# Layer norms of feed-forward and preparation in two stages, with three PSUM banks of their own for the centred values

## The chip, the cores and the metric

The kernel runs on one core of a Trainium2 chip. The metric is the device time of one execution in microseconds (us), as a median of several runs; lower is better. A core has five engines that run side by side, each through its own list of instructions in order: TensorE (PE in the profile, with its weight loads as PEld), VectorE (DVE), ScalarE (ACT), GpSimd (POOL) and SyncE (SP), which here issues all the DMAs. They meet at semaphores. Matrix products are written to PSUM, which has eight banks of 128 x 512 fp32 values; the other tiles lie in SBUF.

## What is computed

Four images of 128 channels and 64 x 64 pixels pass through four layers. The change concerns layer 2, an attention over the 4096 pixels ("tokens") of each image with 16 heads of 8 channels, with a layer norm ahead of it and a small feed-forward behind it:

```python
t = _to_tokens(x)
t = t + _L2_attn_ref(_ln_t(t), ...)

def _L2_attn_ref(x, rx_theta, ry_theta, w_comb, b_comb, w1, b1, w2, b2, g1, beta1, g2, beta2):
    qkv = _qz_ring(heads + rx_theta)          # cosines and their running products
    ...                                       # softmax attention of qkv with itself
    attn_out = ctx @ w_comb.T + b_comb
    x1 = _ln(x + attn_out, g1, beta1)
    zf = jnp.cos(x1[..., :NQ_FFN]) * jnp.cos(ry_theta)
    h = jax.nn.relu(zf @ w1.T + b1)
    ffn_out = h @ w2.T + b2
    return _ln(x1 + ffn_out, g2, beta2)
```

So each token has three norms over its 128 channels: one in preparation (`_ln_t`), two in the feed-forward (`g1`, `g2`).

## The kernel before

**Layout.** Channels lie on the 128 partitions and tokens along the free dimension. An image is worked in NCH = 8 chunks of CH = 512 tokens. A mean over the channels is therefore a matrix product: `layernorm_steps` (L99) multiplies the source by a centring matrix into a PSUM tile `ln_xc` (the source less its mean), squares that on ACT into `ln_sq` (L105), multiplies by a matrix of 1/128 into the PSUM tile `ln_var` (L108), and turns the variance with a 32 x 32 block transpose on DVE into `ln_vt` (L110), so that the square root on ACT (L112, `ln_sd`) and the reciprocal on DVE (L113) need only 16 values in a row. A second transpose spreads the result (`ln_rs`, L115), and DVE multiplies `ln_xc` by it (L118 without a gain, L120 with one; then POOL adds the shift at L121). `ln_xc` keeps its bank until that last product.

`layernorm_steps` is a generator with one `yield` between squaring and `ln_var`. `layernorm` (L92) runs it through at once. Layers 0 and 1 have norms of another kind, layer 3 calls `layernorm` too, in its own pools.

**The order of work.** For each of the four images there is a preparation (`prepare`, L913), the attention itself, and a feed-forward (`feed_forward`, L1223). The loop over b from 0 to 4 runs the feed-forward of image b-1 beside the preparation of image b, then the attention of image b. Both are lists of stages handed to `in_turn` (L797): turn i runs the last stage on the oldest chunk, then the one before it on the next chunk, and so on, with one `yield` after each call, so a chunk passes one stage per turn. `run` takes one call from the feed-forward and one from the preparation alternately.

- Preparation: `fetch` (loads a chunk, `x_in`), `norm` (the norm, and its store to DRAM), `products` (four transposes `tok_t`, the angles `phi`, a cosine of several DVE and ACT instructions into `cs`, and running products on POOL and DVE, L951 to L956), `store` (copies, four transposes `q_t`, splitting, stores). After the chunks, the first heads' queries and keys are loaded.
- Feed-forward: `fetch` (L1226: `den`, `num`, `nrm_in`), `attended` (transposes `den_t`, four DVE steps to a reciprocal, eight small products `rd_ps`, the product `att_ps`, the sum into `nrm_in` at L1256), `first_norm` (into `x1`), `cosines` (product `z_ps` and a cosine `zf`), `hidden` (four PSUM tiles `hid_ps` at once, four Relus at L1277), `sum_up` (eight products `ffn_ps`, the sum `res` at L1287), `last_norm` (norm into `blk`, sum with `x`, store at L1294).

**Buffers and the planner.** A tile pool has `bufs` buffers for each tag; a tile without a tag has its name as tag. For this stretch there is the SBUF pool `l2_mid` (two buffers each unless a tile says otherwise) and the PSUM pool `l2_ps` with eight banks, in which every tile has the tag "mm". In SBUF, `ln_sq` and `ln_vt` share the tag "ln_sq" and so two buffers. The calls set only priorities: a planner places the instructions in each engine's list when their inputs and buffers are there by its reckoning, the earlier in the program first. In the attention, whose pools follow, PE, DVE and POOL keep the written order instead. The attention's tiles take the memory that `l2_mid` leaves.

Of the kernel before, what the change touches and what calls it, by code (L numbers as in the profile page):

```python
# [9 lines left out]
F32 = mybir.dt.float32  # L10
# [5 lines left out]
PSUM = bass.MemoryType.PSUM  # L16

P = 128
# [3 lines left out]
CH = 512  # L22
# [7 lines left out]
class Common:  # L30
# [65 lines left out]
        for _ in self.layernorm_steps(out, src, work, psum, g, b):  # L96
            pass

    def layernorm_steps(self, out, src, work, psum, g=None, b=None):  # L99

        nc = self.nc
        xc = psum.tile([P, CH], F32, name="ln_xc", tag="mm")
        self.mm(xc, self.center, src)
        sq = work.tile([P, CH], F32, name="ln_sq")
        nc.scalar.activation(sq, xc, AF.Square)  # L105
        yield
        vp = psum.tile([P, CH], F32, name="ln_var", tag="mm")
        self.mm(vp, self.mean, sq)  # L108
        vt = work.tile([P, CH // 32, 32], F32, name="ln_vt", tag="ln_sq")
        nc.vector.transpose(vt.rearrange("p a b -> p (a b)"), vp)  # L110
        sd = work.tile([P, CH // 32, 1], F32, name="ln_sd")
        nc.scalar.activation(sd, vt[:, :, 0:1], AF.Sqrt, bias=self.eps5)  # L112
        nc.vector.reciprocal(sd, sd)  # L113
        rs = work.tile([P, CH // 32, 32], F32, name="ln_rs")
        nc.vector.transpose(rs, sd.to_broadcast([P, CH // 32, 32]))  # L115
        rs = rs.rearrange("p a b -> p (a b)")
        if g is None:
            nc.vector.tensor_tensor(out, xc, rs, ALU.mult)  # L118
        else:
            nc.vector.scalar_tensor_tensor(rs, xc, g, rs, ALU.mult, ALU.mult)  # L120
            nc.gpsimd.tensor_scalar(out, rs, b, None, ALU.add)  # L121
# [675 lines left out]
def in_turn(n, *stages):  # L797


    for i in range(n + len(stages) - 1):  # L800
        for k in reversed(range(len(stages))):
            if 0 <= i - k < n:
                stages[k](i - k)
                yield
# [20 lines left out]
def layer2_attention(K, xd, dpool, w):  # L825
# [6 lines left out]
    with ExitStack() as ctx:  # L832
# [81 lines left out]
        def prepare(b, big, two, work, psum):  # L914

            n = NTT * NH * (HD + 1)
            qt = big.tile([P, n + 32], F32, name="qt")
            nc.gpsimd.memset(qt[:, n:], 0.0)  # L920
            values = qt[:, 0:n].rearrange("p (h t d) -> p t h d", h=NH, d=HD + 1)
            nc.gpsimd.memset(values[:, :, :, HD : HD + 1], 1.0)
            shape = [P, 4, NH, HD]
            heads, xs, nrms, laters = {}, {}, {}, {}

            def fetch(c):
                xs[c] = work.tile([P, CH], F32, name="x_in", bufs=3)
                nc.sync.dma_start(out=xs[c], in_=xd[b][:, c * CH : (c + 1) * CH])

            def norm(c):  # L930
                nrms[c] = work.tile([P, CH], F32, name="nrm", bufs=3)
                K.layernorm(nrms[c], xs.pop(c), work, psum)
                nc.sync.dma_start(out=nrm_d[b % 2][:, c * CH : (c + 1) * CH], in_=nrms[c])

            def products(c):

                tp = psum.tile([P, 4, P], F32, name="tok_t", tag="mm")
                for j in range(4):
                    nc.tensor.transpose(tp[:, j, :], nrms[c][:, j * P : (j + 1) * P], K.ident)
                phi = work.tile(shape, F32, name="phi")  # L940
                nc.vector.tensor_tensor(
                    phi.rearrange("p t h d -> p (t h) d"),
                    tp.rearrange("p j (h d) -> p (j h) d", d=HD),
                    theta.unsqueeze(1).to_broadcast([P, 4 * NH, HD]),
                    ALU.add,
                )
                cs = heads[c] = work.tile(shape, F32, name="cs", bufs=3)
                K.cos(cs, phi, work, shape, "cos")
                cc = lambda d: cs[:, :, :, d : d + 1].rearrange("p t h o -> p (t h) o")
                q0 = work.tile([P, 4 * NH, 1], F32, name="q0")  # L950
                nc.gpsimd.tensor_tensor(q0, cc(1), cc(2), ALU.mult)  # L951
                for d in range(3, HD):
                    nc.gpsimd.tensor_tensor(q0, q0, cc(d), ALU.mult)
                for d in range(1, HD):
                    nc.vector.tensor_tensor(cc(d), cc(d - 1), cc(d), ALU.mult)
                nc.vector.tensor_copy(cc(0), q0)  # L956

            def store(c):

                cs = heads[c]  # L960
                nc.scalar.copy(values[:, 4 * c : 4 * c + 4, :, 0:HD], cs)
                j = c // 2
                if c % 2 == 0 and j < NJ - 1:
                    laters[j] = work.tile([P, NH, BT, HD], F32, name="later", bufs=1)
                if j < NJ - 1:
                    at = laters[j][:, :, 4 * (c % 2) : 4 * (c % 2) + 4]
                    nc.gpsimd.tensor_copy(at.rearrange("p h t d -> p t h d"), cs)
                if c % 2 and j < NJ - 1:
                    for q in range(4):
                        nc.sync.dma_start(  # L970
                            out=value_d[:, :, j, q].rearrange("h s t d -> s h (t d)"),
                            in_=laters[j][32 * q : 32 * q + 32].rearrange("s h t d -> s h (t d)"),
                        )
                tp = psum.tile([P, 4, P], F32, name="q_t", tag="mm")
                for j in range(4):
                    nc.tensor.transpose(tp[:, j, :], cs[:, j].rearrange("p h d -> p (h d)"), K.ident)
                tq = work.tile([P, CH], F32, name="tq", tag="phi")
                nc.scalar.copy(tq, tp.rearrange("p j t -> p (j t)"))
                rest = work.tile([P, CH], F32, name="rest", tag="cos_r")
                nc.vector.scalar_tensor_tensor(rest, tq, 4097.0, tq, ALU.mult, ALU.subtract)  # L980
                part = work.tile([P, 2, CH], F32, name="part")
                nc.vector.scalar_tensor_tensor(part[:, 0], tq, 4097.0, rest, ALU.mult, ALU.subtract)
                nc.gpsimd.tensor_tensor(part[:, 1], tq, part[:, 0], ALU.subtract)
                nc.sync.dma_start(
                    out=head_d[:, :, c * CH : (c + 1) * CH].rearrange("z q s -> q z s"), in_=part
                )

            first = []

            def stages():  # L990
                yield from in_turn(NCH, fetch, norm, products, store)
                first.extend(load(0, two))
                for t in first:
                    rounded(t)
                yield

            return stages(), qt, first
# [224 lines left out]

        def feed_forward(b, dsum, work, psum):  # L1223

            loads, x1s, hids, sums = {}, {}, {}, {}

            def fetch(c):
                cols = slice(c * CH, (c + 1) * CH)
                den = work.tile([2 * NH, CH], F32, name="den", bufs=3)
                nc.sync.dma_start(out=den, in_=den_d[:, :, cols].rearrange("p h f -> (p h) f"))  # L1230
                num = work.tile([P, 2, CH], F32, name="num", bufs=3)
                nc.sync.dma_start(out=num, in_=num_d[:, :, cols].rearrange("p q f -> q p f"))
                nrm = work.tile([P, CH], F32, name="nrm_in", bufs=4)
                nc.sync.dma_start(out=nrm, in_=nrm_d[b % 2][:, cols])
                loads[c] = num, den, nrm

            def attended(c):
# [17 lines left out]
                mm(ap, w_comb, num[:, 0])  # L1255
                nc.vector.scalar_tensor_tensor(at, ap, b_comb, at, ALU.add, ALU.add)  # L1256

            def first_norm(c):
                x1 = x1s[c] = work.tile([P, CH], F32, name="x1", bufs=4)
                K.layernorm(x1, loads[c][2], work, psum, g1, beta1)  # L1260

            def cosines(c):
                zp = psum.tile([P, CH], F32, name="z_ps", tag="mm")
# [15 lines left out]
            def sum_up(c):  # L1279
# [6 lines left out]
                r = sums[c] = work.tile([P, CH], F32, name="res")  # L1286
                nc.vector.scalar_tensor_tensor(r, fp, b2, x1s[c], ALU.add, ALU.add)  # L1287

            def last_norm(c):
                o = work.tile([P, CH], F32, name="blk")  # L1290
                K.layernorm(o, sums[c], work, psum, g2, beta2)
                x = loads[c]
                nc.gpsimd.tensor_tensor(x, x, o, ALU.add)
                nc.sync.dma_start(out=xd[b][:, c * CH : (c + 1) * CH], in_=x)  # L1294

            return in_turn(NCH, fetch, attended, first_norm, cosines, hidden, sum_up, last_norm)

        past = None
        for b in range(NB + 1):
            with (  # L1300
# [2 lines left out]
            ):  # L1303
                with (
                    tc.tile_pool(name="l2_mid", bufs=2) as work,
                    tc.tile_pool(name="l2_ps", bufs=8, space=PSUM) as psum,
                ):
                    parts = [feed_forward(b - 1, past, work, psum)] if b > 0 else []
                    if b < NB:
# [449 lines left out]
```

## Time and profile before

| | |
|---|---|
| median of 3 runs | 10960.34 us (10960.1 to 10969.78) |
| profiled execution | 10954.31 us, span 10952.5 us |
| PE busy | 9041.6 us, 83% of the span |
| DVE busy | 7656.5 us, 70% |
| ACT busy | 7514.8 us, 69% |
| POOL busy | 5233.6 us, 48% |
| attention's exponentials (ACT, L1204) | 4932.2 us in 5120 instructions |
| ln_var products, all layers | 240.2 us in 384 instructions, 182.9 us of PE idle before them |

The span is the time from the first to the last instruction of the profiled execution. Most of it, as the row of exponentials shows, is attention. Between its four phases lie the stretches of preparation and feed-forward. In the profile a matrix product of fp32 values appears as two PE instructions. A row of a wait table says which instruction stood idle until which other one was done; in a timeline the number in brackets is that idle time.

### The profile page before, as it was taken

To read this page: it belongs to the slowest core of one execution; us is meant where nothing else is said; L and a number is where in the kernel's file an instruction comes from. 1 tells how busy PE (TensorE), PEld (TensorE's weight loads), DVE (VectorE), ACT (ScalarE), POOL (GpSimd) and SP (SyncE) were. 2 spreads that over 40 slices of the span, in tenths; PEclk is the share of its full clock that TensorE was granted. 3 is DMA by queue.
4 is the path that set the end of the run, shared out by engine and by line. 5 is a ranking of instruction groups with operands and counts; after the bars stand their busy time and mean duration, and the time that the engine had idled before them with its cause. 6 is when DMAs were issued, how large, how long until landed. Compare 5 with 4: busy or idle time off the path is not lost. (4 is left out here: it accounts for less than half of the span.)

```text
span 10952.5 us, 184078 instructions
## 1 busy us (share of the span) xinstructions
PE 9041.6 (83%) x71952; PEld 3464.4 (32%) x71952; DVE 7656.5 (70%) x8462; ACT 7514.8 (69%) x10319; POOL 5233.6 (48%) x3143
## 2 busy tenths in 40 slices
PE   5777778777857999968999968999969999966767
PEld 2223323222332333323333323333323333323333
DVE  2788668668846777757777757777757777744563
ACT  2666565665527999958999948999948999932431
POOL 1565555556624666535665535665535655620000
PEclk8788878877878999979999979999979999977888
DMA  3322322322212222121221222212222212123004
GB/s 83 87 67 57 90 69 56 99 59 59 70 52 40 38 32 34 32 78 35 37 33 33 32 78 38 33 34 33 32 79 39 33 33 34 30 88 96 14 16 139
DMA packets 524327, 581.59 MB, mean 53 GB/s; under 512 B 106233, under 2 KB 329537, under 8 KB 520897
## 3 DMA queue, kind: packets, MB, share of 16 engines
q1 hardware_dynamic: 523456, 569.81, 22.6%
q8 instruction: 568, 9.31, 0.4%
q14 instruction: 303, 2.47, 0.1%
HBM read 373.96 MB, written 76.55 MB: 41 GB/s over the span
## 5 line engine op out<-in xcount | busy, mean ns | idle before, releaser
L1204 ACT ACTIVATE ex<-score 128x1024 f32<-128x1024 f32 x5120 | 4932.2, 1032 | 471.0 <-PE score L90 180.8
L90 PE MATMUL ctx_ps<-ex,qt 128*32 128x512 f32 x20480 | 2719.1, 595 | 0.0
L1151 POOL TENSOR_TENSOR folded<-ex 128x1024 f32<-128x1024 f32 x704 | 1679.4, 2386 | 2073.6 <-ACT ex L1204 2062.0
L1210 DVE STREAM_TRANSPOSE turned<-ex 128x1024 f32<-128x1024 f32 x1536 | 1879.5, 1224 | 470.1 <-ACT ex L1204 426.9
L90 PE MATMUL acc_ps<-turned,turned_v 128*32 128x256 f32 x24576 | 1826.3, 388 | 180.2 <-DVE turned L1190 177.4
L1190 DVE STREAM_TRANSPOSE turned<-ex 128x1024 f32<-128x1024 f32 x1536 | 1854.0, 1207 | 0.0
L90 PE MATMUL score<-queries,keys 32*128 32x512 f32 x10240 | 1359.9, 496 | 120.5 <-ACT ex L1204 74.3
L687 DVE TENSOR_TENSOR_SCAN hs<-decay,carry,hs 128x512 f32<-128x512 f32 x1024 | 1253.0, 1266 | 200.3 <-ACT decay L686 186.0
L686 ACT ACTIVATE decay<-dt,a_neg 128x512 f32<-128x512 f32 x1024 | 701.0, 689 | 788.0 <-DVE hs L687 764.3
L693 POOL TENSOR_TENSOR hs<-hs,c_sb 128x1024 f32<-128x1024 f32 x512 | 1204.9, 2374 | 46.1 <-DMA c_sb<-c_d 26.7
L90 PEld LDWEIGHTS score<-queries,keys 32*128 32x128 f32 x10240 | 524.7, 182 | 2176.5 <-issue 1664.1
L1152 POOL TENSOR_TENSOR quarters<-folded 128x512 f32<-128x512 f32 x704 | 905.1, 1286 | 55.2
L90 PEld LDWEIGHTS acc_ps<-turned,turned_v 128*32 128x32 f32 x24576 | 562.1, 108 | 897.0 <-issue 556.0
L90 PEld LDWEIGHTS ctx_ps<-ex,qt 128*32 128x32 f32 x20480 | 684.0, 110 | 461.0 <-DVE ctx L1133 53.2
L683 DVE TENSOR_TENSOR hs<-dtx,b_ps 128x2048 f32<-128x2048 f32 x256 | 582.2, 2274 | 256.6 <-PE b_ps L90 173.4
L90 PE MATMUL y_ps<-hs,pair 128*64 128x512 f32 x2048 | 644.2, 752 | 137.3 <-POOL hs L693 137.2
L1133 DVE COPY ctx<-ctx_ps 128x512 f32<-128x512 f32 x256 | 177.0, 691 | 669.6 <-PE ctx_ps L90 663.2
L690 POOL COPY carry<-hs 128x4 f32<-128x4 f32 x256 | 59.3, 232 | 1019.7 <-DVE hs L687 976.8
L1023 POOL TENSOR_TENSOR turned_v<-v,quarter 128x1024 f32<-128x1024 f32 x192 | 459.2, 2392 | 18.1 <-DMA v<-value_d 18.1
L1197 DVE TENSOR_REDUCE dacc<-quarters 128x2 f32<-128x512 f32 x704 | 453.4, 644 | 8.0 <-POOL quarters L1152 8.0
L90 PE MATMUL ln_var<-ln_sq,mean 128*128 128x512 f32 x384 | 240.2, 710 | 182.9 <-ACT ln_sq L105 158.1
L90 PE MATMUL b_ps<-dbc,spread 32*128 32x512 f32 x512 | 319.4, 706 | 70.7 <-DVE hs L683 70.7
(353 smaller groups left out, 9684.3 us busy)
## 6 DMA issues: line engine op xcount, KB each, us to landing
c_sb<-c_d SPq DMA_DIRECT2D x512, 128.0 KB
queries<-head_d SPq DMA_DIRECT2D x1024, 64.0 KB
keys<-head_d SPq DMA_DIRECT2D x1024, 64.0 KB
dt<-dt SPq DMA_DIRECT2D x128, 256.0 KB
dtx<-dtx SPq DMA_DIRECT2D x128, 256.0 KB
w<-in_L_ffn_weight SPq DMA_DIRECT2D x32, 1024.0 KB
w<-in_L_ffn_weight SPq DMA_DIRECT2D x128, 256.0 KB
under<-xp SPq DMA_DIRECT2D x384, 66.0 KB
```

What stands on the lines that cost most here:

```text
L90: self.nc.tensor.matmul(out, lhsT, rhs, start=start, stop=stop)
L683: nc.vector.tensor_tensor(hs, dtx2, bb.unsqueeze(1).to_broadcast([P, NQ, CH]), ALU.mult)
L686: nc.scalar.activation(ex, dt2[:, q, :], AF.Exp, scale=a_neg[:, q, g : g + 1])
L687: nc.vector.tensor_tensor_scan(hs[:, q, :], ex, hs[:, q, :], carry[:, g, q : q + 1], ALU.mult, ALU.add)
L693: nc.gpsimd.tensor_tensor(at, at, cs.unsqueeze(1).to_broadcast([P, 2, CH]), ALU.mult)
L1023: nc.gpsimd.tensor_tensor(t, v.unsqueeze(2).to_broadcast([P, 4 * BT, 4, HD]), quarter.unsqueeze(1).to_broadcast([P, 4 * BT, 4, HD]), ALU.mult,
L1151: nc.gpsimd.tensor_tensor(hs, exs[:, :, 0], exs[:, :, 1], ALU.add)
L1152: nc.gpsimd.tensor_tensor(qs, hs[:, :, 0 : CH // 2], hs[:, :, CH // 2 :], ALU.add)
L1190: nc.vector.transpose(*upright)
L1197: nc.vector.tensor_reduce(at, qs, AX.X, ALU.add)
L1204: nc.scalar.activation(ex, sps[p], AF.Exp, scale=scale, accum_out=dacc[:, j, h, t : t + 1] if summed else None)
L1210: nc.vector.transpose(*upright)
```

## The change

Both norms of the feed-forward and the one of the preparation become two stages. The first, one turn earlier, makes `ln_xc` and `ln_sq` and stops at the generator's `yield`; the second takes the generator up and does the rest. Preparation has five stages instead of four, the feed-forward nine instead of seven. `ln_xc` gets a tag "xc" with three buffers in these norms, and the pool's default falls from eight banks to five, so the tag "mm" keeps five. `ln_sq` gets three buffers in these norms, and `ln_vt` a tag of its own with the pool's default of two, in layer 3's norm as well. `num` falls from three buffers to two.

```diff
-    def layernorm_steps(self, out, src, work, psum, g=None, b=None):
+    def layernorm_steps(self, out, src, work, psum, g=None, b=None, tag="mm", bufs=None):
-        xc = psum.tile([P, CH], F32, name="ln_xc", tag="mm")
+        xc = psum.tile([P, CH], F32, name="ln_xc", tag=tag, bufs=bufs)
         self.mm(xc, self.center, src)
-        sq = work.tile([P, CH], F32, name="ln_sq")
+        sq = work.tile([P, CH], F32, name="ln_sq", bufs=bufs)
         nc.scalar.activation(sq, xc, AF.Square)
         yield
         vp = psum.tile([P, CH], F32, name="ln_var", tag="mm")
         self.mm(vp, self.mean, sq)
-        vt = work.tile([P, CH // 32, 32], F32, name="ln_vt", tag="ln_sq")
+        vt = work.tile([P, CH // 32, 32], F32, name="ln_vt")
...
+            def centred(c):
+                nrms[c] = work.tile([P, CH], F32, name="nrm", bufs=3)
+                halves[c] = K.layernorm_steps(nrms[c], xs.pop(c), work, psum, tag="xc", bufs=3)
+                next(halves[c])
+
             def norm(c):
-                nrms[c] = work.tile([P, CH], F32, name="nrm", bufs=3)
-                K.layernorm(nrms[c], xs.pop(c), work, psum)
+                next(halves.pop(c), None)
                 nc.sync.dma_start(out=nrm_d[b % 2][:, c * CH : (c + 1) * CH], in_=nrms[c])
...
-                yield from in_turn(NCH, fetch, norm, products, store)
+                yield from in_turn(NCH, fetch, centred, norm, products, store)
...
-                num = work.tile([P, 2, CH], F32, name="num", bufs=3)
+                num = work.tile([P, 2, CH], F32, name="num", bufs=2)
...
+            def first_centred(c):
+                x1 = x1s[c] = work.tile([P, CH], F32, name="x1", bufs=4)
+                halves[c] = K.layernorm_steps(x1, loads[c][2], work, psum, g1, beta1, tag="xc", bufs=3)
+                next(halves[c])
+
             def first_norm(c):
-                x1 = x1s[c] = work.tile([P, CH], F32, name="x1", bufs=4)
-                K.layernorm(x1, loads[c][2], work, psum, g1, beta1)
+                next(halves.pop(c), None)
...
+            def last_centred(c):
+                sums[c] = sums[c], work.tile([P, CH], F32, name="blk")
+                lasts[c] = K.layernorm_steps(sums[c][1], sums[c][0], work, psum, g2, beta2, tag="xc", bufs=3)
+                next(lasts[c])
+
             def last_norm(c):
-                o = work.tile([P, CH], F32, name="blk")
-                K.layernorm(o, sums[c], work, psum, g2, beta2)
+                next(lasts.pop(c), None)
+                o = sums[c][1]
                 x = loads[c]
...
-            return in_turn(NCH, fetch, attended, first_norm, cosines, hidden, sum_up, last_norm)
+            return in_turn(NCH, fetch, attended, first_centred, first_norm, cosines, hidden, sum_up, last_centred, last_norm)
...
-                    tc.tile_pool(name="l2_ps", bufs=8, space=PSUM) as psum,
+                    tc.tile_pool(name="l2_ps", bufs=5, space=PSUM) as psum,
```

More of the change, by code (lines that the diff above doesn't have):

```diff
@@ L923, in prepare @@
             shape = [P, 4, NH, HD]
-            heads, xs, nrms, laters = {}, {}, {}, {}
+            heads, xs, nrms, laters, halves = {}, {}, {}, {}, {}
             def fetch(c):
@@ L1223, in feed_forward @@
         def feed_forward(b, dsum, work, psum):
-            loads, x1s, hids, sums = {}, {}, {}, {}
+            loads, x1s, hids, sums, halves, lasts = {}, {}, {}, {}, {}, {}
             def fetch(c):
```

## The prediction

> **What bounds the kernel now.** I read the page first. No engine is full over the span (PE 83%, DVE 70%, ACT 69%), and TensorE's granted clock dips to 7 tenths between the long attention phases. There lie the stretches that the change touches, so I asked next for the busy times of each of the five: preparation alone (3185 to 3346), three stretches of feed-forward beside preparation, and feed-forward alone (9609 to 9797).
>
> ```profile
> core 0: us, PE busy (x) PEld busy (x) DVE busy (x) ACT busy (x) POOL busy (x), PEclk, DMA share, GB/s
> 3185.00:3346.00 161.00, 42.49 (x97) 18.62 (x97) 71.25 (x148) 55.69 (x76) 37.44 (x68) 0.56 0.31 79
> 4707.30:4982.30 275.00, 164.18 (x422) 72.42 (x422) 148.05 (x290) 116.32 (x172) 83.67 (x99) 0.74 0.31 85
> 6343.50:6619.00 275.50, 163.84 (x424) 72.13 (x424) 149.73 (x291) 118.13 (x174) 83.18 (x99) 0.76 0.30 86
> 7978.40:8251.00 272.60, 160.47 (x424) 70.73 (x425) 150.64 (x291) 118.28 (x174) 83.11 (x100) 0.76 0.28 87
> 9609.20:9797.00 187.80, 126.54 (x320) 52.54 (x320) 85.98 (x147) 70.75 (x105) 45.80 (x34) 0.77 0.26 83
> ```
>
> Together 1172 us, 10.7% of the span. In a mixed stretch PE works 164 of 275 us and nothing else works longer: it is a chain of waits. The wait table of PE for the first mixed stretch says which:
>
> ```profile
> PE ln_var L90 <- ACT ln_sq L105: 36.7, 24, 8.3
> PE rd_ps L90 <- DVE rc L1248: 30.1, 8, 6.7
> PE q_t L976 <- DVE cs L955: 21.0, 3, 8.5
> PE att_ps L90 <- DVE num L1253: 6.9, 8, 1.3
> PE den_t L1242 <- DMA den<-den_d: 6.7, 1, 6.7
> ```
>
> The columns are total us, times, longest. All 24 norms of the stretch stop PE between their two products. The same row has 35.7 and 33.5 us in the next two mixed stretches, 21.6 (16 times) in feed-forward alone, 12.1 (8 times) in preparation alone: 139.6 us in all. The timeline shows the worst one:
>
> ```profile
> 4768.36 1.02 PE L90 MATMUL ln_xc<-x_in,center 128*128 128x512 f32 x2
> 4777.71 2.08 PE L90 MATMUL ln_var<-ln_sq,mean 128*128 128x512 f32 x2 [8.33 <-ACT ln_sq L105]
> ```
>
> Between the two PE does nothing, though other products were ready. Why? Following PE through 4713 to 4880, its products come exactly in the order of the calls in the program. In layer 3 the same planner leaves that order for one tile only:
>
> ```profile
> 10406.53 1.02 PE L90 MATMUL ln_xc<-x,center 128*128 128x512 f32 x2
> 10407.39 0.83 PE L90 MATMUL kv_sum<-v,e_k 128*128 128x129 f32 x6
> 10408.30 1.12 PE L90 MATMUL ln_var<-ln_sq,mean 128*128 128x512 f32 x2
> ```
>
> kv_sum has a bank of its own and fills the gap; tiles of the tag "mm" never pass one another. So I read the plan as first come, first served within a tag: a product of tag "mm" waits until all earlier ones have their bank. Last, does a stretch's end set the next start? Yes: attention's first exponential waits for the feed-forward's last store.
>
> ```profile
> 4981.06 1.28 ACT L1204 ACT_TABLE_LOAD   x1 [8.46 <-DMA xd<-x]
> ```
>
> **What the Trainium skill says.** "TensorE: Matmul & The Clock Gate", Part 1, has the array at half clock by default and at full clock only after some 3.4 us of sustained work; the trace agrees, since att_ps takes 1141 ns after the rd_ps gap where the same shape takes 592 at best. "PSUM — Partial Sum Buffer", The four PSUM rules: one matmul output fills at most one of eight banks; all tiles here are a bank, so three kept for centred values leave five. "ScalarE: Activation LUTs", What ACT_TABLE_LOAD costs: 1283 ns and a drain of about 1380; the trace has the 1283, but the next instruction starts 1.30 us after the load (4773.52, 4774.82), so I use 1.28. "Perfetto Trace Analysis", Optimization Strategy, warns that repeated bubbles can mean that no buffer is left for the next tile; before, PE shows no wait for a bank, and that is what the change puts at stake.
>
> **The change part by part.** Arithmetic and instruction counts stay; order and buffers move. My sums are against the profiled execution (10954.3, span 10952.5 and 1.8 outside), 6 us below the median of the runs.
>
> *Split of the norm.* In each turn ln_xc and ln_sq now come one turn ahead of ln_var, so ln_var's input is old when PE reaches it. The gates of the expert layers are already split like that; there the wait is at most 0.8 us (5.4 us over 7 waits from 9828 to 9868). Removed in a mixed stretch: 36.7, 35.7, 33.5, mean 35. What is late next is q_t for cs: of the ln_var waits in the two stretches that now end in such a wait (from tok_t at 4817.9 and 4860.5 to q_t) about 3 us come back. Net -32.
>
> *Tag of its own for xc.* ln_xc leaves the "mm" order and goes when its input and one of three banks are there. I listed the calls: every bank is released by a norm call before its next user, but at five of the 24 places (preparation's chunks 4, 6, 7, feed-forward's 5, last norm of 1) only one to three calls before. There PE may meet an ln_xc whose bank DVE has not yet released. From below nothing, from above 2 us each; I take +4. On the other side, ACT and DVE stand in line behind norms that wait: from 4818 to 4830 the cosine chain lost 1.0 (L201 behind ln_sq), 0.8 (L204 behind ln_vt) and 2.6 us (Abs behind a second ln_sq and a table load). With two or three such places a stretch, -6.
>
> *Five banks for all else.* hidden takes four in 1.1 us of PE; they come free with the four Relus, 2.42 us on ACT, starting 1.0 to 2.1 us after hid's first product (4760.7 to 4762.8, 4837.7 to 4839.8). ffn_ps is freed by 0.75 us on DVE. So the second product after hid waits about 1 us, in a chunk. Bounds 0 and 7 (below, rival three). I take 0.75 times 8, +6.
>
> *More turns.* Preparation has 12 turns instead of 11, feed-forward 16 instead of 14. The last chunk's chain (ffn, res, ln_xc, ln_sq, ln_var) is as long as before; filling costs at most one short turn of 8.4 us (the tail's from 4951.8 to 4960.0). I take +4.
>
> *Clock.* ln_var's mean is 775 ns against 592; half of 48 times 0.18 is on the path: -4. att_ps stays slow, for its rd_ps gap stays.
>
> *num with two buffers.* Loads already start when att_ps frees a buffer (4720.72, 4738.47) and land 3.9 us later, a turn ahead of use. One chunk less ahead still leaves more than 10 us: 0. SP's queue holds the same loads behind the same event, so x_in, den and nrm_in behind it on SP meet nothing new. If the cover went, each would cost up to 3.9 us.
>
> *ln_sq three deep, ln_vt with its own two.* It frees the next ln_sq from the older ln_vt; counted in the -6. Layer 3's norm gets it too, 32 times in some 360 us, on an order that PE already fills: 0, at most 3 either way. x, now held one turn longer with three buffers, loads at the latest two turns ahead: 0.
>
> Sum, mixed: -32 + 4 - 6 + 6 + 4 - 4 = -28, three times -84. Feed-forward alone: -21 for its waits, +4 banks, +2 turns, -2 clock: -17; rd_ps (15.1) stays. Preparation alone: its path is tok_t to cs to q_t (12.0 us of a period of 13.6, 3214.7 to 3226.7); of 12.1 us nearly all is beside it, and what goes is tok_t's wait for L118, 8 times 0.5: -4. Total -105: 10849 for the profiled execution, **10855** as a median, 1.0% less.
>
> **The rivals.**
> *One, more than the waits.* If free-running ln_xc also draws rd_ps and q_t forward and the clock holds, 40% of the other 58 us of rd_ps, q_t and att_ps goes: mixed -51, alone -28 and -12: 190 in all, 10770. For it: DVE is only 54% busy in a mixed stretch. Against it: rd_ps needs four DVE steps after den_t, at least 1.75 us.
> *Two, it comes back.* PE's order around the norms may stay (each ln_xc held by its bank until just before its ln_var), or q_t and rd_ps take up the whole gain, DVE's order being what limits: 10950. For it: q_t already has 8.5 us waits. Against: most ln_var waits lie in turns that end without one.
> *Three, slower.* One mechanism: head of line at five banks. If hid's Relus stand on ACT behind a Sin and two table loads with a square root (1.28 + 0.72 + 1.28 + 0.32 = 3.6) and then take 2.42, PE stops some 6 to 7 us a chunk. At 7 in the mixed stretches (56 in place of 6: -28 becomes +22) and 5 in the last (40 in place of 4: +19): 66 + 19 - 4 = +81, 11041. It decides from 34/8 = 4.3 us a chunk. For it: hidden, ffn_ps, tok_t can want six banks at once. Against: Relus start within 2.1 us in the turns I looked at, and the norms held up to three of the eight banks before as well.
>
> **How the numbers follow.** Chances: forecast 0.57, one 0.15, two 0.09, three 0.19. The forecast's own range, with the bounds above (waits regained to 70 or 100%, banks 0 to 1.5 us a chunk, turns 0 to 8), is 10790 to 10920. The whole range must leave out no more than two in ten: half of rival one below 10770, most of rival three above 10975. A measurement here can tell a change of about 0.2%, 22 us. Faster: 0.57 and 0.15, nothing more: 0.72. Same: most of two, 0.08. Slower: 0.20.
>
> **What would show it.** Right: the row ln_var from ln_sq falls below 8 us in each mixed stretch; ln_xc stands apart from its ln_var in PE's order; mixed stretches of 240 to 255 us, the last near 170, the first within 8 of 161. Wrong: rows of PE waiting for ACT hid L1277 (banks) above 30 us a stretch; ln_xc waiting for L118 or L120 above 10; q_t's row grown from 21 to over 45; a stretch not shorter though the ln_var row is gone.

## The result and the profile after

The changed kernel takes 10844.95 us (median of four runs, 10833.8 to 10850.65), the kernel before 10965.06 us beside it (four runs, 10960.1 to 10977.47): a ratio of 0.9891, with a 95% interval of 0.9879 to 0.9903. A second set gave 10836.52 against 10959.83, 0.9892 (0.9876 to 0.9908). The profiled span fell from 10952.5 to 10847.5 us.

To compare stretches I cut every trace at the same events: preparation alone from the last store of the layer before, the others from attention's last reduction (`dsum`), up to attention's first exponential table load, and the last stretch up to layer 3's first load of `x`. Lengths in us, with PE's busy time in it after the slash:

| | layers 0 and 1 | preparation alone | mixed 1 | mixed 2 | mixed 3 | feed-forward alone | what follows it |
|---|---|---|---|---|---|---|---|
| before | 3179.0 | 168.0 | 273.7 / 164.2 | 272.5 / 163.2 | 269.6 / 159.8 | 186.7 / 126.5 | 1156.7 |
| after | 3193.1 | 163.3 | 244.4 / 153.3 | 245.2 / 155.7 | 245.6 / 155.6 | 152.9 / 111.7 | 1155.8 |

The five stretches give 119.0 us back. Layers 0 and 1, whose code is the same, took 14 us longer in this one profile. They vary like that: 3178.8 to 3193.1 over the 14 profiles of this study. The four attention phases take 1360 to 1363 us each, before and after.

The busy times of the changed kernel by stretch (us of the window, then its length, busy time and number of instructions of each engine, PE's granted clock, DMA share and rate):

```profile
core 0: us, PE busy (x) PEld busy (x) DVE busy (x) ACT busy (x) POOL busy (x), PEclk, DMA share, GB/s
3193.14:3356.47 163.33, 41.38 (x102) 20.87 (x102) 69.92 (x161) 53.59 (x74) 39.21 (x68) 0.57 0.33 92
4717.46:4961.81 244.35, 153.29 (x422) 71.47 (x422) 148.48 (x290) 114.80 (x172) 84.68 (x99) 0.76 0.34 96
6324.39:6569.56 245.17, 155.71 (x422) 72.33 (x422) 147.55 (x290) 114.69 (x171) 83.93 (x99) 0.75 0.33 96
7931.55:8177.19 245.64, 155.57 (x422) 72.45 (x422) 147.76 (x290) 114.75 (x172) 83.55 (x99) 0.75 0.34 96
9538.83:9691.75 152.92, 111.66 (x320) 48.66 (x320) 83.28 (x146) 69.96 (x105) 45.77 (x32) 0.84 0.32 100
```

DVE and ACT do the same work in less time; their sums hardly move. PE has as many instructions as before, but in feed-forward alone it is busy 14.9 us less, at a clock of 0.84 instead of 0.77. The rest of the gain is idle time of PE (length less busy time): in the first mixed stretch 109.5 us before, 91.1 after; in feed-forward alone 60.1 and 41.3. PE's wait table for the first mixed stretch says what went and what came:

```profile
PE ln_xc L90 <- DVE ln_rs L120: 24.3, 7, 6.2
PE q_t L980 <- DVE cs L959: 20.5, 4, 7.0
PE rd_ps L90 <- DVE rc L1252: 10.4, 6, 3.7
PE ln_xc L90 <- DVE nrm L118: 6.9, 3, 5.9
...
PE hid_ps L90 <- ACT zf L206: 2.9, 2, 2.2
PE q_t L980 <- ACT hid L1285: 0.7, 1, 0.7
```

The row of ln_var waiting for ln_sq, 36.7 us before, has shrunk to one wait of 0.7 us. A new pair has come instead: ln_xc waits for L118 and L120, the last reads of an older centred value, so for a bank, 31.2 us in ten places. The row of rd_ps has fallen from 30.1 to 10.4, that of q_t stands where it was. The bank wait that rival three was built on, PE held by hid's Relus (now L1285), is 0.7 us.

The timeline of PE has the largest new wait:

```profile
4774.07 1.95 PE L90 MATMUL ln_var<-ln_sq,mean 128*128 128x512 f32 x4
4775.86 1.02 PE L90 MATMUL ln_xc<-nrm_in,center 128*128 128x512 f32 x2
4776.82 0.43 PE L1246 MATMUL den_t<-ident,den 32*128 32x32 f32 x4
4783.45 2.08 PE L90 MATMUL ln_xc<-x_in,center 128*128 128x512 f32 x2 [6.20 <-DVE ln_rs L120]
4785.32 1.91 PE L90 MATMUL rd_ps<-ident,rc 128*128 128x128 f32 x8
```

Two norms' ln_var come together without any wait: their ln_sq are a turn old. Then PE stands for 6.2 us at an ln_xc that waits for its bank. But look at what comes behind it. rd_ps needs rc, and DVE's timeline shows when that was made:

```profile
4782.65 0.75 DVE L120 SCALAR_TENSOR_TENSOR ln_rs<-ln_xc,g,ln_rs 128x512 f32<-128x512 f32 x1
4783.31 0.54 DVE L1250 RECIPROCAL rd<-rd 128x64 f32<-128x64 f32 x1
4783.89 0.57 DVE L1252 COPY rc<-rd 128x512 f32<-128x512 f32 x1
```

The bank came free at 4783.40 and rc was ready at 4784.46. With a free bank, PE would still have stopped at rd_ps until then, for about as long. Much of the 31 us, then, may be the old wait for rc under another name. Whether it is, the experiments had to say.

### The profile page after: what moved, and what is told of

It reads as the page before. It is cut to its first block, busy times and chain, and to the rows that moved or that the text cites. A ratio compares the mean times of both kernels' runs of the same rounds, so it can differ in the third digit from the quotient of the medians.

```text
span 10847.5 us, 184105 instructions
## 1 busy us (share of the span) xinstructions
PE 9021.2 (83%) x71952; PEld 3473.1 (32%) x71952; DVE 7647.7 (71%) x8462; ACT 7513.2 (69%) x10317; POOL 5239.0 (48%) x3143
## 5 line engine op out<-in xcount | busy, mean ns | idle before, releaser
L1208 ACT ACTIVATION_READ_ACCUMULATOR ex<-score 128x1 f32 x1664 | 348.7, 210 | 0.0
```

Of the source, the lines that this page charges most:

```text
L1208: nc.scalar.activation(ex, sps[p], AF.Exp, scale=scale, accum_out=dacc[:, j, h, t : t + 1] if summed else None)
```

## The experiments

The runs e1 to e4 shared one chip, e5 to e11 another, e12 ran on a third, always beside the kernel before. Theory A: each wait of PE costs its length, so the bank waits cost up to 31 us a mixed stretch. Theory B: the gain comes from the tag, which lets ln_xc leave the order of the calls. Theory C: in a mixed stretch the bank waits lie mostly where PE would wait for rc or cs anyway. The lengths, in us (the totals of e1 to e6 are single executions):

| | what differs | mixed 1, 2, 3 | feed-forward alone | total |
|---|---|---|---|---|
| before | | 273.7, 272.5, 269.6 | 186.7 | 10953 to 10965 |
| after | | 244.4, 245.2, 245.6 | 152.9 | 10844.95 |
| e1 | split, eight banks of one tag | 252.5, 251.3, 253.4 | 165.6 | 10876.2 |
| e2 | four banks and four | 246.6, 248.6, 246.2 | 156.2 | 10844.5 |
| e3 | tag, no split | 250.0, 248.9, 252.8 | 176.3 | 10886.4 |
| e4 | x four buffers | 237.5, 238.9, 238.5 | 152.6 | 10836.9 |
| e5 | buffers alone | 267.7, 265.4, 269.0 | 186.4 | 10946.6 |
| e6 | e4, preparation as before | 243.2, 241.3, 242.8 | 158.3 | 10848.7 |
| e7 | e4, preparation's xc in "mm" | 247.4, 248.3, 249.4 | 152.7 | 10856.4 |
| e11 | e4, attended split | 223.1, 218.2, 218.8 | 133.4 | 10746.8 |
| e12 | e11, q_t a turn later | 215.0, 213.1, 211.6 | 134.6 | 10710.8 |

**e1: the split without the banks.** All tiles in eight banks of the tag "mm", the rest of the change kept.

```diff
-halves[c] = K.layernorm_steps(x1, loads[c][2], work, psum, g1, beta1, tag="xc", bufs=3)
+halves[c] = K.layernorm_steps(x1, loads[c][2], work, psum, g1, beta1, tag="mm", bufs=None, sqs=3)
...
-tc.tile_pool(name="l2_ps", bufs=5, space=PSUM) as psum,
+tc.tile_pool(name="l2_ps", bufs=8, space=PSUM) as psum,
```

> The changed kernel's three-stage split with all PSUM tiles in one tag of eight banks again (squares keep three buffers). Theory A (the split alone brings the gain, and the three separate banks cost some 31 us of PE waits for L118 and L120 in each mixed stretch): ln_xc's waits for a bank fall from 31 to under 8 us a mixed stretch, ln_var's stay under 5, mixed stretches 225 to 240 us against 245 of the changed kernel. Theory B (free-running ln_xc in its own tag brings the gain): ln_xc sits in the order of calls again and mixed stretches go back to 260 to 273. Theory C (the waits for a bank only stand where PE would wait for cs or rc anyway): 245 within 3, with the rows of q_t and rd_ps grown by what ln_xc loses. Feed-forward alone: A and C 150 to 156, B 165 to 185.

No bank wait is left, and the mixed stretches are not shorter but 7 us longer than with the change. PE's wait table for the first of them:

```profile
PE rd_ps L90 <- DVE rc L1252: 34.0, 8, 6.5
PE q_t L980 <- DVE cs L959: 33.0, 6, 10.6
PE att_ps L90 <- DVE num L1257: 7.1, 7, 2.3
```

The 31 us of bank waits are back as 23.6 us more for rc and 12.5 more for cs. So they were not a cost on top: theory A falls on the banks. C has the direction, but the stretches lie above its 245 within 3, and feed-forward alone, 12.7 us longer than with the change, is in B's range: leaving the order of the calls is worth something by itself.

**e2: four banks and four.** As the change, with four banks for centred values and four for the rest; ln_sq stays at three buffers.

```diff
-halves[c] = K.layernorm_steps(x1, loads[c][2], work, psum, g1, beta1, tag="xc", bufs=3)
+halves[c] = K.layernorm_steps(x1, loads[c][2], work, psum, g1, beta1, tag="xc", bufs=4)
...
-tc.tile_pool(name="l2_ps", bufs=5, space=PSUM) as psum,
+tc.tile_pool(name="l2_ps", bufs=4, space=PSUM) as psum,
```

> The changed kernel with four banks for centred values and four for all else. Theory A: ln_xc's waits for L118 and L120 fall from 31 to under 12 us a mixed stretch; hidden needs all four other banks, so PE waits for Relus of L1285 and for ffn_ps, 8 to 25 us; mixed stretch 238 to 252, feed-forward alone 155 to 170. Theory C: ln_xc's waits fall but the stretch gains nothing even where no new wait for Relus comes, 245 to 260.

The bank waits of ln_xc fell only to 17.1 and 5.8 us, not below 12, rd_ps's wait rose to 15.6, and the stretches are 0.5 to 3.5 us longer. That lies in the ranges of A and of C, so it doesn't part them; it shows that one bank more for centred values, taken from the rest, gains nothing.

**e3: the banks without the split.** The tag with three banks as in the change, each norm in one stage again, in preparation too.

```diff
-in_turn(NCH, fetch, attended, first_centred, first_norm, cosines, hidden, sum_up, last_centred, last_norm)
+in_turn(NCH, fetch, attended, first_centred, cosines, hidden, sum_up, last_centred)
```

> The changed kernel's banks and buffers, but the norms in one stage again (preparation of four stages, feed-forward of seven). Theory B: the tag alone lets ln_xc go early, so ln_var's waits stay under 10 us and the mixed stretch at 245 within 5. Theory A: ln_xc is freed by a bank only shortly before its ln_var, so waits of ln_var and ln_xc together stay at 30 us or more and the mixed stretch is 258 to 275, feed-forward alone 165 to 185.

The row of ln_var fell to 5.3 us in the first mixed stretch with no split at all: with a bank of its own, ln_xc leaves the order of the calls by itself, and its ln_sq is early. In feed-forward alone 10.1 us of the row stay. The mixed stretches, 249 to 253 us, are at the top of B's 240 to 250 and above it; feed-forward alone, 176.3, is in A's range. Tag and split are two ways to the same end in a mixed stretch; alone, the stretch needs the split.

**e4, e8, e10: four buffers for x.** In the mixed stretches of the change one thing is late that was not before, and its place is the very end. The timeline of the changed kernel there (SPq is SP's DMA queue):

```profile
4942.59 1.89 POOL L912 CAST keys<-keys 128x2048 fp32r<-128x2048 f32 x1
...
4944.43 1.90 POOL L912 CAST queries<-queries 128x2048 fp32r<-128x2048 f32 x1
4944.64 1.12 PE L90 MATMUL ln_var<-ln_sq,mean 128*128 128x512 f32 x2 [0.69 <-ACT ln_sq L105]
...
4946.29 1.26 POOL L1306 TENSOR_TENSOR x<-x,blk 128x512 f32<-128x512 f32 x1
...
4947.57 6.11 SPq L1307 DMA_DIRECT2D xd<-x  x3
...
4954.44 0.46 SPq L1289 DMA_DIRECT2D x<-xd  x1
4954.95 0.66 SPq L903 DMA_DIRECT2D keys<-head_d  x1
4958.09 1.26 POOL L1306 TENSOR_TENSOR x<-x,blk 128x512 f32<-128x512 f32 x1 [4.75 <-issue]
4959.38 0.32 SPq L1307 DMA_DIRECT2D xd<-x  x1
...
4961.81 1.28 ACT L1208 ACT_TABLE_LOAD   x1 [14.93 <-DMA xd<-x]
```

From the last ln_var to attention's table load it takes 17.2 us, in all three mixed stretches. In the kernel before it took 10.6 to 10.7, here up to the table load at 4981.06:

```profile
4970.36 1.13 PE L90 MATMUL ln_var<-ln_sq,mean 128*128 128x512 f32 x2 [0.75 <-ACT ln_sq L105]
```

The x of the last chunk is loaded only at 4954.44, ten microseconds after its norm's ln_var, behind the stores of the three chunks before it (4947.57 to 4953.68), the first of which frees its buffer, because x is held one turn longer now. POOL has a part in it: the first of those stores follows a sum (4946.29) that stands behind the casts of the first heads' keys and queries for attention. The last chunk's sum, its store and attention's first exponential wait for the late x. The edit gives x a fourth buffer and takes the room from den:

```diff
-x = loads[c] = work.tile([P, CH], F32, name="x", bufs=3)
+x = loads[c] = work.tile([P, CH], F32, name="x", bufs=4)
...
-den = work.tile([2 * NH, CH], F32, name="den", bufs=3)
+den = work.tile([2 * NH, CH], F32, name="den", bufs=2)
```

> The changed kernel with x in four buffers (den gets two to make room). If the last chunk's late load of x (issued 4954.44, behind two stores, its sum at 4958.09) is what lengthens the end, attention's first exponential comes 5 to 7 us sooner after the last ln_var (17.2 us now, 10.7 before the change): mixed stretches 238 to 240 us, feed-forward alone 153 within 2, preparation alone unchanged. If another thing holds the end (the stores' place on SP, POOL's casts), mixed stretches stay at 245 within 2.

Each mixed stretch became 6.2 to 7.1 us shorter. Feed-forward alone stayed: there the change, too, loads the last x (9676.55) ahead of its last three stores (from 9682.98). In the timeline of e4 the last loads of x are out early:

```profile
4935.91 1.35 SPq L1289 DMA_DIRECT2D x<-xd  x3
...
4944.63 1.13 PE L90 MATMUL ln_var<-ln_sq,mean 128*128 128x512 f32 x2 [0.69 <-ACT ln_sq L105]
...
4947.51 1.89 POOL L912 CAST keys<-keys 128x2048 fp32r<-128x2048 f32 x1
...
4949.35 1.89 POOL L912 CAST queries<-queries 128x2048 fp32r<-128x2048 f32 x1
4951.20 1.26 POOL L1306 TENSOR_TENSOR x<-x,blk 128x512 f32<-128x512 f32 x1
...
4958.88 1.28 ACT L1208 ACT_TABLE_LOAD   x1 [12.02 <-DMA xd<-x]
```

The tail is 14.3 us in each mixed stretch, 2.9 less than after and still 3.6 more than before, because the two casts have moved behind the last ln_var and the last three sums follow them. It is 14.3 in every run with the casts in that place (e7, e8, e10 and e12 too); in e11 both lie ahead of it again, and it is 11.6.

So less than half of e4's gain is the tail; 3.8 us on average lie ahead of the last ln_var. PE's 422 instructions come in the same order in both kernels. In the first mixed stretch, counted from its start, e4 is 1.3 us ahead at one q_t, whose cs is ready sooner. Another 2.3 us come at the products some 20 us later, from an att_ps to an ln_var, which take longer in the change (the att_ps 1.06 us against 0.59). The other two stretches show the same two steps. The late load of x does not explain them; their cause stays open.

Since one execution can't carry 8 us, it was timed again, and then beside the changed kernel on one chip:

> The kernel of e4 again, in rounds: the change with x four buffers and den two. The theory that x's three buffers delay the last chunk by some 6.5 us in each mixed stretch: 10820 to 10838, ratio to before 0.9870 to 0.9888, and below the change's 10845. The rival that e4's single look was luck: 10842 to 10850.

> The changed kernel itself, on the same chip as the next two: 10840 to 10850 us, ratio to before 0.988 to 0.990.

> The kernel of e4 and e8 beside the changed one. If x's fourth buffer is worth the 6.5 us of each mixed stretch that its timeline shows: 10822 to 10834, 12 to 22 us below the run of the changed kernel in this call, mixed 237 to 240. If the difference between e8 and the change was that of two chips: within 6 us of the changed kernel.

e8 gave 10826.98 (ratio 0.9876, 0.986 to 0.9893). In the last set the changed kernel (e9) took 10836.52 (10830.3 to 10848.01) and the one with four buffers (e10) 10819.38 (10811.83 to 10826.48): 17 us less, every run of it below every run of the other, and within the 12 to 22 expected. Both medians lie some 3 us below the ranges expected for them. The three mixed stretches are 25.6 us shorter together in these two profiles, preparation alone 3.8 and feed-forward alone 2.7 longer. The tail gives 2.8 of the 8.5 us of a stretch.

**e5: the buffers alone.** The kernel before, with ln_sq three deep, ln_vt with its own two, and num with two.

```diff
-sq = work.tile([P, CH], F32, name="ln_sq")
+sq = work.tile([P, CH], F32, name="ln_sq", bufs=bufs)
...
-vt = work.tile([P, CH // 32, 32], F32, name="ln_vt", tag="ln_sq")
+vt = work.tile([P, CH // 32, 32], F32, name="ln_vt")
...
-num = work.tile([P, 2, CH], F32, name="num", bufs=3)
+num = work.tile([P, 2, CH], F32, name="num", bufs=2)
```

> The kernel before with only the changed buffers: ln_sq three deep, ln_vt with two of its own, num with two; norms whole, all tiles in eight banks of one tag. Theory A (the buffers give nothing by themselves; the gain is the split and the tag): mixed stretches 268 to 275 us, feed-forward alone 184 to 189, the ln_var row of PE 35 to 38 us in the first mixed stretch, total within 12 us of before. Theory B (ln_vt in line for ln_sq's buffers holds the norms back, as my term of -6 a stretch had it): mixed 262 to 267, feed-forward alone 178 to 183, total 25 us less.

Between the two: the mixed stretches lost 6.1, 7.1 and 0.6 us, 4.6 on average, and feed-forward alone nothing. ln_var's row in the first mixed stretch shows where it came from, 36.7 before:

```profile
PE ln_var L90 <- ACT ln_sq L105: 26.3, 24, 3.8
```

A cost of num's third buffer doesn't show, but it was not taken away alone, so a small one could hide in the gain of the others. With e5 as the base, split and tag can be told apart. Averages of the three mixed stretches: split -14.9 (e1), tag -16.8 (e3), both -22.3 (after). Feed-forward alone: -20.7, -10.1 and -33.5. They overlap in the mixed stretches, where preparation runs beside the feed-forward, and add up where it does not.

**e6 and e7: preparation taken out of the three banks.** Both have x's fourth buffer, so they stand against e4. In e6 preparation's norm is whole, in "mm"; in e7 it is split, in "mm".

```diff
-halves[c] = K.layernorm_steps(nrms[c], xs.pop(c), work, psum, tag="xc", bufs=3)
+halves[c] = K.layernorm_steps(nrms[c], xs.pop(c), work, psum, sqs=3)
```

> Only the feed-forward's norms are split and use the three banks of their own; preparation's norms are whole in the other five; x has four buffers, den two, as in e4. Theory C (preparation's norms gain only because they are off the order of the calls; their wait comes back): PE's ln_var row 10 to 14 us in the first mixed stretch, mixed 243 to 250 against 238 of e4, feed-forward alone 152 to 154, preparation alone 166 to 169, total 10850 to 10870. Theory D (two kinds of norm taking turns for three banks cost as much as the split of preparation's gains): ln_xc's bank waits fall from 31 to under 10 us and mixed stays at 235 to 240, total 10825 to 10840.

> Both norms split, but preparation's centred values in the five banks in order of the calls, only the feed-forward's in the three; x four buffers, den two. Theory D (mixing two kinds of norm in the three banks costs): ln_xc's bank waits fall below 12 us and mixed to 230 to 235, total 10815 to 10830. Theory C (bank waits lie where PE would wait for cs and rc anyway): mixed 237 to 243, the q_t and rd_ps rows take up what the ln_xc rows lose, total 10833 to 10850.

In e7 the bank waits fell to 5.1 us, as wanted, and the mixed stretches grew by 10 us; rd_ps waits 34.6 us there. Theory D, that two kinds of norm in three banks cost, is wrong. C has the direction, but its 237 to 243 was too good: e7 also takes the free order from preparation's ln_xc. That this order is worth those 10 us is not shown, since e6 takes it away too, with preparation's norm whole, and is only 4 us longer than e4 in the mixed stretches, with a tail 2.6 us shorter. C's row of 10 to 14 us for ln_var came out as 3.9 in e6. Its feed-forward alone, 158.3 with no preparation beside it, fits no theory here; 3.7 of the 5.7 us over e4 are longer busy time of PE, and why stays open.

**e11: the same thing done to the other wait.** If waiting in the order of the calls is the trouble, the four DVE steps from den_t to rc should gain from a turn of their own too.

```diff
-            def attended(c):
-                num, den, at = loads[c]
+            def shares(c):
+                den = loads[c][1]
...
+            def attended(c):
+                num, den, at = loads[c]
+                rc = rcs.pop(c)
...
-in_turn(NCH, fetch, attended, first_centred, first_norm, cosines, hidden, sum_up, last_centred, last_norm)
+in_turn(NCH, fetch, shares, attended, first_centred, first_norm, cosines, hidden, sum_up, last_centred, last_norm)
```

> As e4, and the denominators' half of attended (den_t to rc) one turn ahead of rd_ps, so that PE's wait for rc is handled as the change handles the wait for ln_sq. Theory C (waits of PE are exchangeable in the mixed stretches, where the vector and scalar engines' chains set the pace, but add up in feed-forward alone): rd_ps row from 10 to under 3 us in the first mixed stretch and from 14 to under 3 in feed-forward alone; mixed 232 to 239 (gain at most half of the row), feed-forward alone 140 to 145, total 10805 to 10825. Theory A (each wait of PE that goes shortens the stretch by as much): mixed 225 to 229, feed-forward alone 138 to 140, total 10780 to 10800. The rival that the extra turn and the longer life of num take it back: total 10825 to 10840.

10746.8 us (ratio 0.9807, 0.9793 to 0.9821), 73 us below e10 on the same chip and better than every expectation. The windows of the first mixed stretch and of feed-forward alone, and PE's wait table for the former:

```profile
4716.84:4939.94 223.10, 145.41 (x422) 67.15 (x422) 146.26 (x290) 110.48 (x168) 83.15 (x99) 0.79 0.36 105
...
9462.77:9596.19 133.42, 101.95 (x320) 45.00 (x320) 83.46 (x146) 69.64 (x105) 45.26 (x32) 0.89 0.36 115
```

```profile
PE q_t L980 <- DVE cs L959: 36.5, 8, 8.5
...
PE ln_xc L90 <- DVE nrm L118: 5.9, 4, 2.5
PE att_ps L90 <- DVE num L1261: 4.9, 3, 3.3
...
PE ln_xc L90 <- DVE ln_rs L120: 3.2, 3, 1.7
```

The wait for rc is down to 1.8 us, and with it have gone most of the bank waits of ln_xc, 31.2 us in the change and 9.1 here, though the three banks are as they were. That shows what the reading of 4783 suggested: those bank waits were in the main the wait for rc. q_t takes 16 us of it back, as C says. But C gave the stretch at most half of the row, and against e10 the three lose 13.8 to 20.0 us: 8.5 to 8.8 us of idle time, nearly all of the row (11.3 to 1.8 in the first), as A has it, and 5.0 to 11.5 us of busy time of PE. In feed-forward alone the length falls by 19.4 us, 9.2 of them busy time. Neither theory had counted this shorter busy time.

**e12: and to q_t.** An empty stage between preparation's products and store.

```diff
-in_turn(NCH, fetch, centred, norm, products, store)
+in_turn(NCH, fetch, centred, norm, products, turned, store)
...
+            def turned(c):
+                pass
```

> As e11, and an empty stage between preparation's products and store, so that q_t reads a cs that is one turn old. If PE's waits on other engines' results are what sets these stretches, whichever tile they fall on: q_t's row from 36.5 to under 12 us in the first mixed stretch, mixed 200 to 210, preparation alone 135 to 155 (before 170), feed-forward alone 131 to 136 as in e11, total 10660 to 10710. If the vector and scalar engines' lines set the mixed stretches by now, so that PE's waits only move: q_t's row goes to ln_xc, att_ps or tok_t, mixed 214 to 222, preparation alone 160 to 170, total 10730 to 10755.

10710.83 us (10704.94 to 10719.83), ratio 0.9774 (0.9761 to 0.9787), the best of this study and faster than both kernels. Preparation alone came to 152.1 us, as the first theory had it; the mixed stretches went to 213 on average, near the second, whose 214 to 222 they just undercut; the total lies just above the first's 10660 to 10710. PE's wait table for the first of them:

```profile
PE ln_xc L90 <- DVE nrm L118: 17.3, 3, 7.6
PE q_t L983 <- DVE cs L959: 11.0, 2, 5.6
PE ln_xc L90 <- DVE ln_rs L120: 7.7, 4, 4.8
```

q_t lost 25.5 us of waiting, ln_xc took up 15.9, and the stretch gained 8.1. By now most of what PE stops waiting for in one place it waits for in another.

## Why the prediction came out right

The forecast of 10855 us lies 10 us above the measured median. Its direction, its main mechanism (the wait of ln_var goes) and the lengths of the mixed stretches held (240 to 255 was forecast, 244 to 246 came). The last stretch did not, 153 for a forecast near 170, and several terms inside did not either; that they cancelled in part is luck.

- **The split, -32 a mixed stretch.** Removal right: 36.7 us to 0.7. What is late next was named wrong. q_t's row stayed at 20 to 21; the waiting moved to ln_xc's banks. Measured alone, the split is worth 15 us (e1 against e5), because the tag does part of the same.
- **The tag, +4.** A miss in sign: alone it is worth -17 (e3 against e5), and on top of the split still -7 (after against e1). I had foreseen bank waits at five places of at most 2 us; there were ten of up to 6.2, 31 us in all. By my own list of signs ("ln_xc waiting for L118 or L120 above 10") that would have spoken against the forecast. It did not, as e1 and e11 show: the banks held PE where rc would have. The sign was badly chosen, since a row of waits has a price only together with what would be late in its place.
- **ACT and DVE in line, with ln_sq's and ln_vt's buffers, -6.** e5 has -4.6 for the buffers alone. (One of the three readings behind it was short: from L203's end to L204 the chain lost 1.5 us, not 0.8.)
- **Five banks, +6, and rival three.** The Relus held PE for 0.7 us in the first mixed stretch. The term is about 0, and rival three had no ground: 34 us of such waits were its threshold.
- **More turns, +4, and x at 0.** An end that is later did come, 6.5 us, but from x's third buffer and POOL's casts, not from the turns: in e11, with four buffers and a turn more, it is 11.6 us, 0.9 more than before. "x, now held one turn longer with three buffers, loads at the latest two turns ahead: 0" is a step that failed; it overlooked the last chunk, whose load stands on SP behind three stores that come in one bunch, at the place that sets attention's start. Its price is 2.9 us a stretch where the casts then fall into the end (e4). The whole gain of e4 and e10, 6.7 and 8.5 us a stretch, is more than that price. (The turn read from 4951.8 to 4960.0 is 8.3 us, not 8.4.)
- **Clock, -4 in a mixed stretch.** PE was busy 10.9, 7.4 and 4.2 us less, 7.5 on average. (ln_var's mean before was 730 to 764 ns in the three stretches, not 775; the term stays.)
- **Mixed in sum.** -28 forecast; -29.4, -27.3 and -23.9 measured. Of these 19.3 on average are idle time of PE, where the terms gave 24.
- **Feed-forward alone, -17.** -33.7 measured, so half was missed. The idle part was close: -15 by the terms (waits, banks, turns), -18.9 measured, and "rd_ps (15.1) stays" held with 13.8. The term that failed is the clock: -2 against 14.9 us less busy time. I had counted only the change's own ln_var, which gives 2.6 of it; rd_ps gives 2.9. "att_ps stays slow", said of the mixed stretches, was wrong there (a mean of 1141 ns before, 916 after in the first) and here, where it gives 2.8. The groups of instructions (count, busy us, mean ns, idle time before them), before and then after:

```profile
L90 PE MATMUL att_ps<-num,w_comb 128*128 128x512 f32 x16 | 16.6, 1141 | 6.5 <-DVE num L1253 6.5
```

```profile
L90 PE MATMUL att_ps<-num,w_comb 128*128 128x512 f32 x16 | 13.8, 963 | 6.0 <-DVE num L1257 3.4 <-ACT zf L206 1.8 <-issue 0.8
```

- **Preparation alone, -4.** -4.7 in this pair. Six profiles with the changed preparation (after, e4, e8 to e11) took 161.2 to 169.5 us, three with the norm whole in "mm" (before, e5, e6) 168.0 to 171.0: right on average (-4.1), unclear in a single profile.
- **num and layer 3, 0.** Nothing speaks against it: e5 shows no cost of num's two buffers, and what follows the last stretch took 1156.7 and 1155.8 us, in a spread of 1145 to 1160 over all profiles.
- **The agreement of the profiled sums is luck.** -105 was forecast and -105.0 measured in the one profile, but that holds the 14 us by which layers 0 and 1 ran longer; the stretches gave 119, and the medians 120.

Rival one had a true core. rd_ps, q_t and att_ps together fell from 58 to 35 us in the first mixed stretch, the 40% it named; but bank waits took their place, and its 51 us became 29. Rival two was half true as well: PE was held by its banks, yet the gain stayed.

What stays open: what sets a mixed stretch once rc and cs are ahead. DVE is busy 147 of 215 us in e12's first, ACT 117, so no engine is full; that it is the chains through both, each in its own order, is argued and not shown. Open, too, is what of e4's gain lies ahead of the last ln_var.

## What to carry to other kernels

When PE stops between two products of one chunk because another engine works in between, put a turn of other work between them, and do it to every such wait: after the 120 us of this change, the second and third such step (e11, e12) brought 73 and 36 more. Before pricing a new wait, look for what would be late in the same place without it; and when a stage makes a tile live a turn longer, follow the last chunk to the end of its stretch, where no later turn hides its load.

## What the hardware showed beyond that

With shorter idle times PE's own work became shorter. In feed-forward alone the same 320 instructions took 126.5 us at a granted clock of 0.77 before, 111.7 at 0.84 after, and 102.0 at 0.89 in e11. That agrees with the Trainium skill, "TensorE: Matmul & The Clock Gate", Part 1, by which the clock is granted for sustained work and withdrawn when PE idles. Removing idle time there took away 8 to 9 us of busy time with each 10 us of idle (14.9 with 18.9, then 9.2 with 10.1). The mean clock alone doesn't tell the busy time, though: in the same stretch e1 has 117.0 us at 0.78 and e2 116.3 at 0.85, and in the first mixed stretch e1 has 150.4 at 0.73, the change 153.3 at 0.76. So the clock as the only cause is not shown.
